# A two-layer transformer block on one core: token rows dispatched by a table of slots, an opening with routing among the wide products, and a first pass with seven inner products for three of seven weights

## The chip, the cores and the metric

The kernel runs on one core of one Trainium2 chip. The metric is the device time of one execution in microseconds (us), and the median of several runs is given. Everything is 32-bit floating point. The engines are named as in the profile: PE is TensorE (PEld its weight loads), DVE is VectorE, ACT is ScalarE, POOL is GpSimd, and SP is SyncE, which issues most DMAs.

## The reference

The block has two layers over 8 x 256 tokens of 512 channels. In outline:

```python
xn = layernorm(x)
x  = x + L0_attention(xn) + L0_experts(xn)
xn = layernorm(x)
x  = x + L1_attention(xn) + L1_low_rank(xn)
```

L0_attention is a decaying linear attention with 32 heads of 128: `qkv = silu(xn @ qkv_w.T)`, scores of each head times a decay, the result divided by its root mean square, times `norm_w`, times `sigmoid(xn @ gate_w.T)`, and projected by `out_w`. L0_experts is

```python
gate = top-2 of 16 experts, chosen within the best 2 of 4 groups
y = sum over experts e of gate[:, e] * (silu(xn @ w1[e] + b1[e]) * (xn @ w2[e] + b2[e]) @ w3[e] + b3[e])
z = silu(xn @ sw1 + sb1) * (xn @ sw2 + sb2) @ sw3 + sb3          # shared, for all tokens
```

L1_attention is a softmax attention with one head of 128 per sequence. L1_low_rank picks 16 of 64 rank-16 pairs for each token and sums their outputs with softmax weights.

## The kernel before, in words

The 2048 tokens are handled as 4 chunks (index i, NCH = 4) of 512 tokens, each of 4 tiles of 128 (index t).

**The opening** (up to `opening.close()`, L525) normalises every chunk (`begin`, L417), turns its tiles by TensorE transposes (`turn_rows`, L240), forms on POOL the sums of token blocks that the later products need (`token_sums`, L369; stored to xc, for chunk 0 kept on chip as first_x), computes the shared expert's first half (`shared_up`, L317: 16 products with 512 columns, L312), the routing (`route`, L265: 16 narrow products into ps_sc at L271, then a chain of DVE instructions), decay tables (L359) and, one chunk later, the shared expert's second half (`shared_down`, L329). In `shared_down` the chunk's gates, with a 17th column of ones, are turned by TensorE (L333), copied to geT, and multiplied with b3_t (17 x 512, the experts' biases and the shared one, L338), so that all output biases are added there; two products a tile (L340) follow. `clear` writes zeros over xd, a DRAM array with one row of 512 for every slot (47 tiles of 128 slots). After the last chunk the slot of each token's two experts is counted (L447 to L523), on DVE and with three TensorE products.

**The attention of layer 0** runs over 4 chunks x 8 groups of 4 heads. One (chunk, group) is a unit. The products of a unit are formed by a two-level scheme with seven instead of eight products: seven outer products (ORDER = p1, p2, p6, p5, p3, p7, p4), each with its own sum of weight blocks w and of token blocks x. In chunks 1 to 3 each outer product is again done with seven inner products of four 128-column matmuls (`p1` to `p7` in class Outer, `product` L661), whose operands are sums made earlier. In chunk 0, the first pass, it is done plainly (`plain`, L981): four quarters of two products, eight in all. During the first pass, POOL also makes the inner sums of each weight (`inner_sum`, L634) and stores them to DRAM (ws), from where the later chunks load them; the outer sums (p6, p5, p3, p7) are made on DVE (`outer_sum`). p1, p2 and p4 (RAW) use weights as they come. A weight tile is 8 x 512 columns (`big`, a ring of three buffers); `prepare(n + 2)` loads the weight of the outer product after next, and `following.step` runs one sum of the next weight after each product.

**Order.** Within the attention, ACT and POOL execute in the order of the code; for PE, DVE and SP a planner sets the order from its own costs. Besides, the code counts slots: `slot()` advances after a product (49 a unit), and `later(n, f)` puts a piece of other work n slots ahead. Pieces are the scores, the attention, the output projection, the routed experts (`expert`), and in the first pass the dispatch (`row`, `scatter`): a normalised tile is loaded from xnd, and POOL writes its rows by two indirect DMAs to their slots in xd. From chunk 1 on, each of 47 expert tiles loads its rows from xd (L696, on SP) and its expert's weights by an indirect DMA (L697, on POOL), turns the rows (8 slots later), does the first half (11) and the second (14); ACT copies the result and SP stores it to yd (L733, L734). `load_sum` (L933) fetches x plus the shared expert of a chunk when its last group is nearly done, and `finish` adds the attention to it.

**Layer 1** begins with `wrapped_up` (L1145), which gathers chunk 0's expert rows, adds and normalises them during the last units. `Head` (L1302) does routing and attention, `seven` the low-rank products.

Of the kernel before, what the change touches and what calls it, by code (L numbers as in the profile page):

```python
# [9 lines left out]
FP = mybir.dt.float32  # L10
I32 = mybir.dt.int32
# [55 lines left out]
def block_kernel(  # L67
# [75 lines left out]
    def once(shape, name):  # L143
        return work.tile(shape, FP, tag=name, name=name, bufs=1)

    scratch = big("scratch").rearrange("p (h b) n -> p h (b n)", h=4)
    xs = [work.tile([P, TPC, C], FP, tag="x", name=f"x{i}", bufs=NCH) for i in range(NCH)]
    x_t = x.rearrange("(i t p) c -> i t p c", t=TPC, p=P)
    for t in range(TPC):
        nc.sync.dma_start(out=xs[0][:, t, :], in_=x_t[0, t])  # L150
# [14 lines left out]
    b3_t = held[0 : E + 1, SH * C : (SH + 1) * C]  # L165
    nc.sync.dma_start(out=b3_t, in_=b3)
# [8 lines left out]
    xd = dram.tile([NSLOT, C], FP, name="xd")  # L175
# [7 lines left out]
    xnd = [dram.tile([P, TPC, C], FP, name=f"xnd{i}") for i in range(NCH)]  # L183
# [5 lines left out]
    zero = held[:, (SH + 1) * C : (SH + 2) * C].unsqueeze(1)  # L189
    nc.gpsimd.memset(zero, 0.0)  # L190

    ident = const.tile([P, P], FP, name="ident")
    make_identity(nc, ident)
    eps_t = const.tile([P, 1], FP, name="eps_t")
    nc.gpsimd.memset(eps_t, EPS)
# [5 lines left out]
    before = once([P, E, E], "before")  # L201
# [8 lines left out]
    dist = const.tile([P, S + P], FP, name="dist")  # L210
# [15 lines left out]
    def normalize(o, xc):  # L226

        mv = small.tile([P, TPC, 2], FP, tag="mv", name="mv")
        for t in range(TPC):
            st = small.tile([P, 6], FP, tag="st", name="st")  # L230
            nc.vector.bn_stats(st, xc[:, t, :])
            nc.vector.bn_aggr(mv[:, t, :], st)
        rstd = small.tile([P, TPC], FP, tag="rstd", name="rstd")
        rsqrt(rstd, mv[:, :, 1])
        for t in range(TPC):
            nc.vector.tensor_scalar(
                o[:, t, :], xc[:, t, :], mv[:, t, 0:1], rstd[:, t : t + 1], ALU.subtract, ALU.mult
            )
# [26 lines left out]
    def route(xT, ge, sel):  # L265

        full = [P, TPC, E]
        pl = ps_sc()
        for t in range(TPC):
            for c in range(NC):  # L270
                mm(  # L271
                    pl[:, bass.ts(t, E)], xT[:, c, bass.ts(t, P)], rw[:, c, :],
                    start=(c == 0), stop=(c == NC - 1),
                )
# [31 lines left out]
        tt(ge[:, :, 0:E], sc, sel, ALU.mult)  # L306
        nc.vector.memset(ge[:, :, E : E + 1], 1.0)
# [9 lines left out]
    def shared_up(i):  # L317
        hT = scratch[:, 2 + i % 2, :].rearrange("p (e n) -> p e n", e=SH)
        for e in range(SH):
            p1, p2 = ps_mm(), ps_mm()  # L320
            project(p1, wsh, e, i)
            project(p2, wsh, SH + e, i)
            h1 = work.tile([P, CH], FP, tag="h1", name="h1")
            b1, b2 = bsh_t[:, 0, e : e + 1], bsh_t[:, 1, e : e + 1]
            nc.scalar.activation(h1, p1, AF.Silu, bias=b1)
            nc.vector.scalar_tensor_tensor(hT[:, e, :], p2, b2, h1, ALU.add, ALU.mult)
        return hT

    def shared_down(i, hT):  # L329
        xc = xs[i]  # L330
        pg = ps_sc()
        for t in range(TPC):
            nc.tensor.transpose(pg[0 : E + 1, bass.ts(t, P)], gates[i][:, t, :], ident)  # L333
        gT = work.tile([E + 1, CH], FP, tag="geT", name="geT", bufs=1)
        nc.scalar.copy(gT, pg[0 : E + 1, :])
        for t in range(TPC):
            py = ps_mm()
            mm(py, gT[:, bass.ts(t, P)], b3_t, start=True, stop=False)  # L338
            for e in range(SH):
                mm(py, hT[:, e, bass.ts(t, P)], w3sh[:, e, :], start=False, stop=(e == SH - 1))  # L340
# [4 lines left out]
    sel_all = once([P, NTT, E], "sel_all")  # L345

    def share(i, hT):
        shared_down(i, hT)
        nc.sync.dma_start(out=xr[i], in_=xs[i])
# [17 lines left out]
    first_x, first_w = {}, []  # L367

    def token_sums(i):  # L369
# [18 lines left out]
        for p, at in (  # L388
# [9 lines left out]
            if i == 0:  # L398
                if y is not with_:
                    nc.sync.dma_start(out=blocks(first_x[p][:, 0:4]), in_=y)  # L400
# [9 lines left out]
    def clear(i):  # L410
        lo, hi = (0, 12, 24, 36, NMT)[i : i + 2]
        nc.sync.dma_start(
            out=xd[lo * P : hi * P, :].rearrange("(j p) c -> p j c", p=P),
            in_=zero.to_broadcast([P, hi - lo, C]),
        )

    def begin(i):  # L417
        xns.append(work.tile([P, TPC, C], FP, tag="xn", name=f"xn{i}"))
        normalize(xns[i], xs[i])
# [3 lines left out]
    for i in range(NCH):  # L423
# [3 lines left out]
        nc.sync.dma_start(out=xnd[i], in_=xns[i])  # L427
# [8 lines left out]
        ups.append(shared_up(i))  # L436
        ge = once([P, TPC, E + 1], f"ge{i}")
        route(xT[i], ge, sel_all[:, bass.ts(i, TPC), :])
        gates.append(ge)
        decays(i)  # L440
        clear(i)
# [8 lines left out]
    disp = Parts(accp.tile([P, 7 * CH], FP, tag="acc", name="disp"))  # L450
# [50 lines left out]
    nc.vector.tensor_reduce(own, owner, AX.X, ALU.add)  # L501
    nc.vector.tensor_scalar(own, own, float(E - 1), float(P), ALU.min, ALU.mult)
# [14 lines left out]
    for n in range(TOP):  # L517
        tt(hit, slot, ends_[:, n, :].unsqueeze(2).to_broadcast(full), ALU.is_equal)
        tt(hit, hit, sel_all, ALU.mult)
        for i in range(NCH):  # L520
            at_i = bass.ts(i, TPC)
            tt(hit[:, at_i, :], hit[:, at_i, :], gates[i][:, :, 0:E], ALU.mult)
# [72 lines left out]

    def spare8():
        return staged("spare")[:, 0 : TPC * C].rearrange("p (t c) -> p t c", t=TPC)

    with tc.tile_pool(name="attn", bufs=1) as attn, tc.manual_schedule(engines={mybir.EngineType.Activation, mybir.EngineType.Pool}):
# [5 lines left out]
        def weights(i, g, p, steps):  # L605
# [14 lines left out]
            if i == 0:  # L620
# [13 lines left out]
                def inner_sum(f, o, a_, b_):  # L634
                    f(w[:, o], w[:, a_], w[:, b_], pool)
                    if o == 7:
                        nc.sync.dma_start(out=ws[g][p], in_=w[:, 4 if p in RAW else 1 : 8])

                if outer:
                    steps += [partial(outer_sum, n) for n in (1, 2, 0, 3)]  # L640
                steps += [
                    partial(inner_sum, *at) for at in ((add, 4, 0, 3), (sub, 5, 4, 1), (sub, 6, 2, 5), (sub, 7, 1, 0))
                ]
# [978 lines left out]
```

## Time and profile before

| | |
|---|---|
| median of 3 runs | 2861.57 us (2854.19 to 2862.28) |
| the profiled execution | 2856.16 us, its span 2854.4 us |
| granted PE clock over the span | 0.993 |
| opening, until the first product of L666 | 164.4 us |
| first pass (chunk 0), about | 598 us |
| chunks 1 to 3 and layer 1 | from 762 us on |
| DMA | 763.21 MB, 267 GB/s on average |

The span runs from the first to the last instruction of the program in one profiled execution. Busy time is what an engine's instructions take; PE's records overlap[...], so a row of them is priced from start to start. One fp32 matmul of 512 columns shows as two records.

### The profile page before, as it was taken

To read this page: it belongs to the slowest core of one execution; us is meant where nothing else is said; L and a number is where in the kernel's file an instruction comes from. 1 tells how busy PE (TensorE), PEld (TensorE's weight loads), DVE (VectorE), ACT (ScalarE), POOL (GpSimd) and SP (SyncE) were. 2 spreads that over 40 slices of the span, in tenths; PEclk is the share of its full clock that TensorE was granted. 3 is DMA by queue.
4 is the path that set the end of the run, shared out by engine and by line. 5 is a ranking of instruction groups with operands and counts; after the bars stand their busy time and mean duration, and the time that the engine had idled before them with its cause. 6 is when DMAs were issued, how large, how long until landed. Compare 5 with 4: busy or idle time off the path is not lost. (4 is left out here: it accounts for less than half of the span.)

```text
span 2854.4 us, 49572 instructions
## 1 busy us (share of the span) xinstructions
PE 2796.7 (98%) x19864; PEld 2566.1 (90%) x19864; DVE 1569.7 (55%) x2615; ACT 948.2 (33%) x1683; POOL 1465.7 (51%) x1213
## 2 busy tenths in 40 slices
PE   8989999999999999999999999999999999999999
PEld 4469999999999999999999999999999999987877
DVE  6555666666654445444545555555555555556663
ACT  3312222212244333333443333443444333432221
POOL 4545666665546555555645454545544566552210
PEclk9999999999999999999999999999999999999999
DMA  7888998899986777778877777777777788652211
GB/s 255 301 309 337 357 352 341 341 349 347 364 320 246 262 266 273 282 270 299 296 265 257 264 266 265 259 274 280 284 259 259 267 310 298 222 212 88 76 61 61
DMA packets 161943, 763.21 MB, mean 267 GB/s; under 512 B 18209, under 2 KB 24225, under 8 KB 109874
## 3 DMA queue, kind: packets, MB, share of 16 engines
q1 hardware_dynamic: 149826, 706.25, 66.9%
q0 software_dynamic: 11888, 53.79, 5.2%
q8 instruction: 157, 2.57, 0.4%
q14 instruction: 72, 0.59, 0.1%
HBM read 596.14 MB, written 163.05 MB: 266 GB/s over the span
## 5 line engine op out<-in xcount | busy, mean ns | idle before, releaser
L666 PE MATMUL ps_a<-xt,w 128*128 128x128 f32 x5376 | 750.9, 276 | 11.7 <-DVE r L97 7.7
L666 PEld LDWEIGHTS ps_a<-xt,w 128*128 128x128 f32 x5376 | 681.9, 192 | 30.1 <-issue 14.3
L97 POOL TENSOR_TENSOR c<-c 128x512 f32<-128x512 f32 x216 | 271.7, 1273 | 262.0 <-DVE c L97 259.9
L97 POOL TENSOR_TENSOR c<-c,r 128x512 f32<-128x512 f32 x240 | 318.4, 1347 | 158.9 <-DVE r L97 153.1
L666 PE MATMUL ps_e<-xt,w 128*128 128x128 f32 x2688 | 373.4, 275 | 1.3 <-DVE c L97 1.3
L97 POOL TENSOR_TENSOR sums<-sums,sq 128x512 f32<-128x512 f32 x120 | 153.3, 1278 | 426.4 <-ACT sq L796 425.6
L996 ACT COPY cp<-ps_a 128x512 f32<-128x512 f32 x336 | 196.4, 585 | 476.0 <-PE ps_a L666 468.8
L666 PEld LDWEIGHTS ps_e<-xt,w 128*128 128x128 f32 x2688 | 344.4, 192 | 11.2 <-issue 3.8
L97 POOL TENSOR_TENSOR w<-w 128x512 f32<-128x512 f32 x224 | 294.6, 1325 | 108.2 <-issue 31.2
L666 PE MATMUL ps_a<-w,xt 128*128 128x128 f32 x1792 | 346.7, 275 | 0.0
L858 PE MATMUL ps_sc<-wo,gT 128*128 128x256 f32 x1288 | 305.1, 379 | 1.8 <-POOL gT L97 1.8
L97 DVE TENSOR_TENSOR acc<-ps_sc,acc 128x512 f32<-128x512 f32 x208 | 143.3, 690 | 265.8 <-PE ps_sc L858 198.8
L666 PEld LDWEIGHTS ps_a<-w,xt 128*128 128x128 f32 x1792 | 272.3, 192 | 0.0
L97 DVE TENSOR_TENSOR c<-ps_a,c 128x512 f32<-128x512 f32 x232 | 157.9, 686 | 202.7 <-PE ps_a L666 201.7
L858 PEld LDWEIGHTS ps_sc<-wo,gT 128*128 128x128 f32 x1288 | 232.3, 190 | 26.8 <-POOL gT L97 2.0
L666 PE MATMUL ps_b<-xt,w 128*128 128x128 f32 x1680 | 236.4, 277 | 6.8 <-ACT c L1010 4.2
L801 DVE SCALAR_TENSOR_TENSOR gT<-ps_o,nw,c 128x256 f32<-128x256 f32 x256 | 112.0, 479 | 231.0 <-ACT sq L796 222.0
L666 PEld LDWEIGHTS ps_b<-xt,w 128*128 128x128 f32 x1680 | 217.3, 194 | 17.5 <-issue 8.2
L744 ACT ACTIVATE c<-c 128x512 f32<-128x512 f32 x256 | 148.9, 627 | 170.1 <-DVE c L97 170.0
L796 ACT ACTIVATE sq<-ps_o 128x512 f32<-128x512 f32 x120 | 71.6, 597 | 382.3 <-PE ps_o L782 382.3
L666 PE MATMUL ps_e<-w,xt 128*128 128x128 f32 x896 | 173.2, 275 | 0.0
L97 DVE TENSOR_TENSOR s<-ps_sc,decay 128x384 f32<-128x384 f32 x256 | 139.8, 552 | 40.7 <-PE ps_sc L770 38.1
(299 smaller groups left out, 4635.8 us busy)
## 6 DMA issues: line engine op xcount, KB each, us to landing
w<-in_w_att_dram SPq DMA_DIRECT2D x128, 1024.0 KB
st<-in_w_att_dram SPq DMA_DIRECT2D x32, 1024.0 KB
wo<-in_w_out_dram SPq DMA_DIRECT2D x113, 256.0 KB
decay<-dec SPq DMA_DIRECT2D x64, 384.0 KB
w<-ws0p SPq DMA_DIRECT2D x12, 1792.0 KB
w<-ws1p SPq DMA_DIRECT2D x12, 1792.0 KB
w<-ws2p SPq DMA_DIRECT2D x12, 1792.0 KB
w<-ws3p SPq DMA_DIRECT2D x12, 1792.0 KB
```

The costliest lines, as they stand in the source:

```text
L97: (eng or nc.vector).tensor_tensor(o, a, b, op)
L666: mm(bank[:, bass.ts(ty, P)], a, b, start=(first and ty == 0), stop=True, skip_group_check=True,)
L744: nc.scalar.activation(qk, qk, AF.Silu)
L796: nc.scalar.activation(sq, po, AF.Square)
L801: nc.vector.scalar_tensor_tensor(gT[:, h, :].rearrange("p (t n) -> p t n", t=2), po[:, bass.ts(h, S)].rearrange("p (t n) -> p t n", t=2), ...
L858: mm(py[:, bass.ts(t, S)], self.O[p][:, hh, bass.ts(t, P)], self.wo[p][:, hh, :], start=(t == 0 and hh == 0), stop=(hh == 1), skip_group_c ...
L996: nc.scalar.copy(c, bank)
```

## The change

1. **Dispatch.** The array xd and its clearing go. xnd becomes one array of 2048 rows; a new DRAM array `table` (one 32-bit number for each slot, declared last) is set to 0, and in the first pass POOL scatters token numbers into it: 32 indirect DMAs of 128 numbers in place of 16 row loads and 32 scatters of rows. At the last unit of the pass `read_table` loads the table, and TensorE turns it (`whose`). Each expert tile then gathers its rows from xnd by an indirect DMA on POOL.
2. **Biases.** b3_t, the gates' transposes and the product L338 go. An expert tile gathers its bias row by another indirect DMA (own_, 12 slots after its begin) into the place of its rows, and DVE adds it to the product (before: a copy on ACT). Pieces lie at 10, 12, 13 and 18 slots instead of 8, 11 and 14. The shared bias is added by `last_bias`: a load and four POOL adds for each chunk.
3. **Opening.** The loads of chunk 0 alternate between the queues of SP and ACT, its tiles are normalised one at a time, an early square root and 16 transposes of the identity are added, the routing's products stand between the shared expert's (`between`), and the next chunk is turned ahead of this chunk's decays and of `share`. sel_all, before and the gates move into disp (the space of acc), dist into the opening's pool.
4. **First pass.** p1, p2 and p4 use seven inner products, as the later chunks do; p6, p5, p3 and p7 stay plain (`sevenfold`). The inner sum for p7 is made first, and the token sums of chunk 0 for these three are made by 12 POOL instructions on 128 x 128 blocks (`first_sums`). A seven's last product, `p3`, stands after the next outer product's first two, or ahead of a plain one.
5. **Layer 1.** `wrapped_up` normalises in pieces, and the first head's routing products stand between those of q and k (`opening`).

```diff
-    b3_t = held[0 : E + 1, SH * C : (SH + 1) * C]
-    nc.sync.dma_start(out=b3_t, in_=b3)
-        nc.sync.dma_start(out=xs[0][:, t, :], in_=x_t[0, t])
+        (nc.scalar if t % 2 else nc.sync).dma_start(out=xs[0][:, t, :], in_=x_t[0, t])
...
+    table = dram.tile([NSLOT, 1], I32, name="table")
+    none = once([NMT, P], "none", I32)
+    nc.gpsimd.memset(none, 0)
+    nc.sync.dma_start(out=table.rearrange("(j p) o -> j (p o)", p=P), in_=none)
...
+    nc.scalar.activation(root[:, 0:1], eps_t, AF.Sqrt)
+    for _ in range(2):
+        idle = ps_o()
+        for n in range(WARM):
+            nc.tensor.transpose(idle[:, bass.ts(n % 4, P)], ident, ident)
...
         for t in range(TPC):
-            nc.tensor.transpose(pg[0 : E + 1, bass.ts(t, P)], gates[i][:, t, :], ident)
-        gT = work.tile([E + 1, CH], FP, tag="geT", name="geT", bufs=1)
-        nc.scalar.copy(gT, pg[0 : E + 1, :])
-        for t in range(TPC):
             py = ps_mm()
-            mm(py, gT[:, bass.ts(t, P)], b3_t, start=True, stop=False)
...
+        pl, tiles = ps_sc(), list(range(TPC))
+        ups.append(shared_up(i, lambda: scores(pl, xT[i], tiles.pop(0))))
+        ge = disp.tile([P, TPC, E], FP, name=f"ge{i}")
+        route(pl, ge, sel_all[:, bass.ts(i, TPC), :])
         gates.append(ge)
+        if i + 1 < NCH:
+            turn(i + 1)
         decays(i)
-        clear(i)
...
+    def last_bias(r, t3):
+        nc.sync.dma_start(out=t3, in_=b3[E : E + 1].to_broadcast([P, C]))
+        for t in range(TPC):
+            add(r[:, t, :], r[:, t, :], t3, nc.gpsimd)
...
                 steps += [
-                    partial(inner_sum, *at) for at in ((add, 4, 0, 3), (sub, 5, 4, 1), (sub, 6, 2, 5), (sub, 7, 1, 0))
+                    partial(inner_sum, *at) for at in ((sub, 7, 1, 0), (add, 4, 0, 3), (sub, 5, 4, 1), (sub, 6, 2, 5))
                 ]
+                if p in RAW:
+                    return sums_of(w)
...
+        for t in first_sums:
+            sub(t[:, 4], t[:, 1], t[:, 0], nc.gpsimd)
+            sub(t[:, 1], t[:, 3], t[:, 1], nc.gpsimd)
+            sub(t[:, 5], t[:, 3], t[:, 4], nc.gpsimd)
+            sub(t[:, 6], t[:, 2], t[:, 5], nc.gpsimd)
...
-                nc.sync.dma_start(out=self.xe, in_=xd[bass.ts(j, P), :])
+                nc.gpsimd.indirect_dma_start(
+                    out=self.xe, out_offset=None, in_=xnd[:, :],
+                    in_offset=bass.IndirectOffsetOnAxis(ap=whose[:, j : j + 1], axis=0),
+                    bounds_check=NT - 1, oob_is_err=False,
+                )
...
+            def bias(self):
+                nc.gpsimd.indirect_dma_start(
+                    out=self.xe, out_offset=None, in_=b3[:, :],
+                    in_offset=bass.IndirectOffsetOnAxis(ap=own_[:, self.j : self.j + 1], axis=0),
+                    bounds_check=E, oob_is_err=False,
+                )
...
-                nc.scalar.copy(ye, py)
+                add(ye, py, self.xe)
...
+                    last_bias(self.r, attn.tile([P, C], FP, tag="sum", name="sb3", bufs=3))
...
             def go(self, bank, p, first=False):
                 product(bank, self.w[p], self.x[p], first)
                 slot()
+                if self.following:
+                    self.following.step()
...
-            later(8, e.turn)
-            later(11, e.up)
-            later(14, e.down)
+            later(10, e.turn)
+            later(12, e.bias)
+            later(13, e.up)
+            later(18, e.down)
...
+        def sevenfold(n):
+            return plan[n][0] > 0 or plan[n][2] in RAW
...
-                    for e in range(2):
-                        later(1 + 24 * e, partial(row, 2 * g + e))
+                    for e in range(5 * g, min(5 * g + 5, TOP * NTT)):
+                        later(5 + 10 * (e - 5 * g), partial(scatter, e // TOP, e % TOP))
+                    if g == NG - 1:
+                        later(4, read_table)
...
-            if i == 0:
+            last = outers[n - 1] if n and sevenfold(n - 1) else None
+            if not sevenfold(n):
+                if last:
+                    last.p3()
                 prepare(n + 2)
                 cur.plain(outers[n + 1])
                 continue
+            if i == 0:
+                while cur.steps:
+                    cur.step()
+                cur.following = outers[n + 1]
             cur.p1()
             cur.p7()
-            if plan[n - 1][0] > 0:
-                outers[n - 1].p3()
+            if last:
+                last.p3()
             prepare(n + 2)
```

## The prediction

> **What bounds the kernel now.** I read the page first, then the busy time by stage (cut where the records change code lines), TensorE's list of waits, and the records themselves in time order.
>
> ```profile
> span 2854.4 us, 49572 instructions
> PE 2796.7 (98%) x19864; PEld 2566.1 (90%) x19864; DVE 1569.7 (55%) x2615; ACT 948.2 (33%) x1683; POOL 1465.7 (51%) x1213
> ```
>
> TensorE is busy 98%, the next engine 55%. Removed matmuls are therefore worth about their time, if their feeders keep up. By stage (columns: window, length, busy us and instructions of PE, PEld, DVE, ACT, POOL, granted clock, DMA share, GB/s):
>
> ```profile
> 0.00:164.40 164.40, 144.23 (x439) 73.60 (x439) 96.32 (x201) 53.09 (x79) 81.94 (x129) 0.94 0.75 279
> 164.40:762.00 597.60, 584.73 (x4527) 564.38 (x4526) 371.37 (x587) 128.71 (x222) 351.05 (x275) 0.99 0.90 344
> 762.00:1457.00 695.00, 692.09 (x5286) 657.38 (x5285) 347.48 (x538) 276.39 (x498) 383.63 (x302) 1.00 0.77 285
> ```
>
> The opening idles 20 us, the first pass 13 (most of it in its first unit), the second 3. The waits (total us, times, longest) name the places:
>
> ```profile
> PE ps_b L243 <- DVE xn L236: 10.2, 1, 10.2
> PE ps_b L666 <- ACT c L1010: 4.2, 1, 4.2
> PE ps_sc L333 <- DVE ge L97: 3.6, 1, 3.6
> ```
>
> TensorE's records in time order (start, duration): eight wide records (L312) take 5.44 us from start to start early on and 3.43 soon after; the L338 pairs further down are those that the change removes:
>
> ```profile
> 13.66 5.14 PE L271 MATMUL ps_sc<-rw,xT 128*128 128x16 f32 x24
> 18.63 5.60 PE L312 MATMUL ps_b<-xT,wsh 128*128 128x512 f32 x8
> 24.07 3.60 PE L312 MATMUL ps_a<-xT,wsh 128*128 128x512 f32 x8
> 27.50 3.60 PE L312 MATMUL ps_e<-xT,wsh 128*128 128x512 f32 x8
> ...
> 131.91 1.12 PE L338 MATMUL ps_b<-held,geT 17*128 17x512 f32 x2 [0.67 <-ACT geT L335]
> 132.96 1.98 PE L340 MATMUL ps_b<-held,scratch 128*128 128x512 f32 x4
> 134.87 1.12 PE L338 MATMUL ps_a<-held,geT 17*128 17x512 f32 x2
> ```
>
> Prices are start to start, since records overlap: L312 3.43 us per eight, L338 1.05 per pair, L340 1.91 per four.
>
> **The Trainium skill.** "TensorE: Matmul & The Clock Gate", Part 1: the array starts at half clock and is released after about 3.4 us of activity. The trace agrees in kind (the first transposes come every 0.22 us, later ones every 0.11), although its clock column says 1.00 there. "DMA: Bandwidth & Descriptors", Anatomy of one DMA: a GpSimd-issued DMA costs about 2.0 us plus bytes over 436 GB/s, an estimate of 2.6 us for 256 KB. The trace disagrees: 256 KB row gathers (L556) land after a median 6.2 us, row scatters (L1094) after 7.3. "ScalarE: Activation LUTs", What ACT_TABLE_LOAD costs: 1283 ns; the trace shows 1.28 us at 7.68, on the chain to the first transpose.
>
> **The opening (−45 us).** Removed: the biases b3 through TensorE. 16 pairs x 1.05 = 16.8; 16 gate transposes, about 4 x 0.45 = 1.8; their waits on geT (2.0) and ge (3.6). Added ahead: x on two queues, statistics, root and scaling per tile, a table load done early, 16 idle transposes. The statistics of the last tile of x began at 6.72; with 0.69 + 0.18 + 0.30 + 0.18 + 0.54 and hand-overs it is scaled near 9, turned and copied near 10. The wide products, which need the 1 MB w_sh issued at 4.09, started at 18.63; I put them at 10 (x and w_sh, 2 MB at the 287 GB/s of that stretch from about 2.5, is 9.8). What remains for TensorE: L312 16 x 3.43 = 54.9; L340 16 x 1.91 = 30.6; scores 4 x 1.71 = 6.8; transposes of three chunks 5.3; counting 1.7: 99.3, so 109.3 with no idle. Cold stretches and waits were about 28 us here; turning a chunk ahead and scores between products take most of those at 36 to 43, 74 to 85 and 147 to 155. I keep 10: the opening ends at 119, 45 earlier. DVE still has 95 us of work there, so it becomes nearly as tight as TensorE. The 12 MB clearing of xd goes (DMA share 0.75, so worth nothing by itself, but the xsum stores behind it held POOL 47.5 us). If DVE's cover fails, the opening is DVE's, which is rival 2. The set-up edits (table, none, own_, token, dist's place, the order of memsets) are records of 0.1 to 0.5 us on POOL and DVE and two 24 KB transfers, beside a first transpose that waits for x anyway: nothing. ACT issues two of the x loads ahead of its first work.
>
> **Entry into the first pass (−5 us).** ACT's first copy of c waited for DVE's counting to 175.33, for its memory was the opening's; sel_all, before and the gates now lie in disp. That returns most of the 4.2 us wait, the 1.7 us on w at 186.7 and a cold 1.5. Of 7.4 I take 5, since p6's 3 MB must still come.
>
> **The first pass (−13 us).** By the diff only p1, p2 and p4 get seven products, not all seven outer ones: one of 8 products, 3 x 8 times. A product is 0.89 us (563.42 to 564.32), so 24 x 0.89 = 21.4. ACT and DVE gain 6 copies and 3 adds a unit (3.5 and 2.1 us), POOL 6 adds (7.8 of about 47 busy in 74.5, plus twelve small sums once): hidden by idle time (uncovered, POOL's would be 8 x 7.8 = 62 us). But products now need POOL's inner sums of w, which were only stored before. Worst is p4 (first pass, sixth unit, whose p1 begins at 537.64 and the next at 612.09: 74.45 us; SPq rows are issues):
>
> ```profile
> 589.31 6.36 SPq L622 DMA_DIRECT2D w<-in_w_att_dram  x2
> 599.74 5.21 POOL L97 TENSOR_TENSOR w<-w 128x512 f32<-128x512 f32 x4 [2.85 <-issue]
> 602.32 0.83 PE L666 MATMUL ps_b<-xt,w 128*128 128x128 f32 x6
> ```
>
> Its load waits for a buffer whose store ends at 589.3, and lands at 599.7; the sums p7 and p6 need are ready at 601.0 and 603.7, while TensorE reaches p4 at 602.32 and, 1.8 us less for p1 and p2, would want them near 601.4 and 602.6. A last product after the next two also returns p4's buffer about 0.9 us later. Against this, 2 row loads and 4 scatters a unit (1.5 of about 26 MB: 344 GB/s x 74.5 us) become 512-byte scatters: some 2 us off the 39 us of DMA in this ring. I take a stall of 1 us a unit: 8 x (2.7 − 1) = 13. Bounds 0 and 21.4. Scatters no longer wait for a row on POOL.
>
> **Passes two to four (+5 us).** Each of 47 tiles gets two more indirect DMAs on POOL, and loses one load on SP:
>
> ```profile
> L697 POOL DMA_INDIRECT xw<-in_w_exp_dram,rows__1106 x47: 1005/1011/1053, 764.0 to 2211.2; - x47
> ```
>
> 94 x 1.0 us lies in POOL's idle 45%. The result's bias add moves from ACT (0.58) to DVE (0.69), 32 us on an engine half idle. The new wait: the bias gather is issued 12 slots after the tile's begin, needed at 18. A unit of 49 slots takes 73.1 us, 1.49 a slot, so 9 us for a landing of 6 to 7.5 plus POOL's delay (0 to 5 us: L697 at 1072.26 followed ten back-to-back POOL records). DVE then waits up to about 3 us for some tiles, with the sc bank held and every product's eviction queued behind; TensorE is late when its a, b and e banks are all unread. Bounds 0 and 117 (47 x 2.5); I take 5. On POOL the gather also waits for the tile's own transposes, two slots before it. The later turn (10 for 8) gives the token gather time.
>
> **Shared bias, closing (0).** last_bias: a 256 KB load and four POOL adds of 1.27 before finish, four times; its t3 needs a sum buffer, on SP, and POOL's c adds queue behind. The 1 MB r was issued at 768.3 and used at 801, so only t3 can be late: 0 to 5 each, I take +3 in all. Splitting the normalisation in wrapped_up takes the 2.6 us wait at 2443, and interleaving ranks with q and k some of the 0.4 there: −3.
>
> **Sum.** −45 − 5 − 13 + 5 + 3 − 3 = −58. The profiled execution took 2856.16 (span 2854.4 and 1.8 around it): 2798. The median is 5.4 above it, so 2804.
>
> **Rivals.** (1) All of it: no cold stretch (−52), full 21, no costs: about 2780. For it: POOL and DVE have the time; against: the p4 lines. (2) Feeders bind: DVE's chain of chunk after chunk ends the opening at 138 (−26) and the ring of three weight buffers keeps the first pass at 74.5 us a unit (0): about −26, 2835. For it: DVE 96 us of 119, DMA 0.90 in the pass; against: 12 and 12.6 MB less to move. (3) Slower: the bias gather stops DVE in Expert.down. From 58/47 = 1.2 us a tile it eats the gain; at 2.5 the time is about 2920. For: landings up to 13.0 us at L697; against: the 256 KB gathers landed within 8.9 us at worst, and POOL waits for others half its time, so is mostly on time. That all seven outers take the seven form is only the title; the code leaves four plain.
>
> **How the numbers follow.** Forecast 0.52, rival 1 0.13, rival 2 0.20, rival 3 0.12 (nearly all slower), small mixtures near no change 0.03. Forecast and rivals 1 and 2 span 2780 to 2835; with the bounds of the opening (±8) and runs (8 us apart before) 2768 to 2846, which leaves out 0.15. Differences under 0.3% (8.6 us) can't be told from none: faster 0.84, same 0.03, slower 0.13.
>
> **What would show it.** Right: no L338-like records; first wide product near 10 and first pass product near 119; units of the first pass near 73 us; the remaining stages within 10 us of 2093. Wrong: TensorE waiting for POOL's w at p4; DVE waiting for the bias gather; POOL held in last_bias; an opening that ends past 135 with DVE as releaser.

## The result, and the profile after

The changed kernel takes 2941.73 us (median; 2934.31 to 2950.83). The kernel before, run beside it, takes 2861.58 us (2854.19 to 2862.28). The ratio is 1.0288, with a 95% interval of 1.0252 to 1.0323: it is slower by 80 us, where the forecast was 2804 us. The profiled execution took 2938.48 us.

The page's head (the span, then busy time, share and instructions of each engine):

```profile
span 2936.8 us, 49479 instructions
PE 2777.3 (95%) x19641; PEld 2560.4 (87%) x19641; DVE 1641.1 (56%) x2689; ACT 947.0 (32%) x1682; POOL 1651.0 (56%) x1383
```

TensorE is busy 19 us less than before (2796.7) in a span that is 82 us longer. The removed matmuls are gone; what was added is mostly idle time, and in part matmuls that take longer (the first experiment separates the two). The busy time by stage shows where. The columns are the window, its length, busy us and instructions of PE, PEld, DVE, ACT and POOL, granted clock, DMA share, and GB/s. The stages here are cut at the first product, at the first gather of an expert's weights (the first slots of the second pass), and at the last product.

```profile
0.00:131.90 131.90, 114.45 (x401) 65.06 (x401) 96.75 (x193) 48.85 (x77) 87.71 (x141) 0.95 0.72 268
131.90:828.80 696.90, 595.43 (x4376) 568.38 (x4377) 402.62 (x628) 157.23 (x272) 417.20 (x326) 0.93 0.93 276
828.80:2609.60 1780.80, 1755.68 (x13363) 1671.63 (x13362) 952.69 (x1427) 677.46 (x1207) 1072.63 (x858) 1.00 0.76 278
```

Cut at the same marks, the kernel before has 164.4, 599.6, 1768.3 and, from the last product on, 322.1 us. The changed kernel has 131.9, 696.9, 1780.8 and 327.2. So the opening gave 32.5 us, the first pass took 97.3, the other passes 12.5 and the rest 5.1.

In the first pass the DMA share rose from 0.90 to 0.93 while the rate fell from 344 to 276 GB/s. The DMA engines are no less busy and deliver a fifth less. TensorE's list of waits (total us, times, longest) says what it lacks:

```profile
PE ps_a L710 <- DMA w<-in_w_att_dram: 46.5, 6, 10.2
PE ps_a L710 <- DVE w L98: 13.4, 6, 5.5
PE ps_o L844 <- DVE s L98: 11.1, 5, 7.6
PE ps_b L710 <- DVE w L98: 9.4, 1, 9.4
PE ps_sc L779 <- DVE xeT L763: 9.0, 7, 1.3
```

None of these was among the waits that the prediction showed of before. The first, second and fourth are for weights that are late, or for sums made from them; the third lies in the same stage. All fall in the first pass except the fifth, which is in the second.

One answer on the records of the new scatter names a suspect. Its lines give the duration (in ns), the idle time of POOL for an earlier scatter that had not landed (us, times), and the time from issue to landing:

```profile
L1156 POOL DMA_INDIRECT table<-token,slots x32: 992/993/1699, 143.6 to 704.3; - x32
  DMA table<-token,slots: 25.3, 6
DMA to landing us min/median/max: 9.7/11.1/13.8
```

512 bytes take 11.1 us to land. A scatter of 256 KB of rows in the kernel before took 7.3 (L1094):

```profile
DMA to landing us min/median/max: 6.7/7.3/8.2
```

The trace also records every DMA packet. In the changed kernel 461 packets take over 2.5 us, together 1706 us, or 107 us for each of the 16 DMA engines. In the kernel before there are 3, together 8 us. 411 of the 461 begin 3 to 9 us after a scatter, though these stretches are 192 of the 561 us from the first scatter to the last, and every one of the 32 scatters has some. After the scatter at 253.12 us, for instance, 16 packets of 14336 bytes begin between 258.73 and 258.88 and take 2.9 to 6.5 us each; the mean of that size in the first pass of the kernel before is 0.56.

### The profile page after: what moved, and what is told of

Its sections match the earlier page's. It is cut to its first block, busy times and chain, and to the rows that moved or that the text cites. A ratio compares the mean times of both kernels' runs of the same rounds, so it can differ in the third digit from the quotient of the medians.

```text
span 2936.8 us, 49479 instructions
## 1 busy us (share of the span) xinstructions
PE 2777.3 (95%) x19641; PEld 2560.4 (87%) x19641; DVE 1641.1 (56%) x2689; ACT 947.0 (32%) x1682; POOL 1651.0 (56%) x1383
## 4 chain that ended last, share of the span: by engine, by line
PE 71%; DMA 14%; DVE 8%; issue 4%; POOL 3%; SPq 0%; ACT 0%; DVEq 0%; POOLq 0%; ACTq 0%
PE ps_a L710 20%; PE ps_e L710 10%; PE ps_sc L921 9%; PE ps_b L710 5%; DMA st<-in_w_att_dram 4%; PE ps_o L844 3%; PE ps_sc L832 3%; PE ps_sc L779 3%; DMA w<-in_w_att_dram 3%; PE ps_sc L941 2%; PE ps_a L1633 2%; DVE w L98 2%; PE ps_o L845 2%; PE ps_sc L833 1%; DVE r L98 1%
## 5 line engine op out<-in xcount | busy, mean ns | idle before, releaser
L710 PE MATMUL ps_a<-xt,w 128*128 128x128 f32 x5376 | 762.1, 278 | 74.9 <-DMA w<-in_w_att_dram 46.5
L710 PEld LDWEIGHTS ps_a<-xt,w 128*128 128x128 f32 x5376 | 695.0, 194 | 103.5 <-issue 59.6
L98 POOL TENSOR_TENSOR c<-c 128x512 f32<-128x512 f32 x240 | 302.5, 1276 | 263.1 <-DVE c L98 254.0
L98 POOL TENSOR_TENSOR c<-c,r 128x512 f32<-128x512 f32 x264 | 347.7, 1337 | 174.0 <-DVE r L98 171.7
L1063 ACT COPY cp<-ps_a 128x512 f32<-128x512 f32 x384 | 224.1, 584 | 659.1 <-PE ps_a L710 631.7
L710 PE MATMUL ps_b<-xt,w 128*128 128x128 f32 x1536 | 218.6, 279 | 21.0 <-DVE w L98 9.4
L98 DVE TENSOR_TENSOR c<-ps_a,c 128x512 f32<-128x512 f32 x216 | 146.9, 687 | 144.7 <-PE ps_a L710 138.9
L710 PEld LDWEIGHTS ps_b<-xt,w 128*128 128x128 f32 x1536 | 199.3, 195 | 29.7 <-issue 27.8
```

The lines of the kernel that those rows point to most:

```text
L98: (eng or nc.vector).tensor_tensor(o, a, b, op)
L710: mm(bank[:, bass.ts(ty, P)], a, b, start=(first and ty == 0), stop=True, skip_group_check=True,)
L1063: nc.scalar.copy(c, bank)
```

## Experiments: what stopped the first pass

Three theories stood at first. Theory S: the scatters of single numbers hold up every DMA beside them. Theory P: the arrays lie elsewhere in DRAM now and collide. Theory R: the form of seven waits for POOL's sums and the ring of three weight buffers. Four kernels ran on one chip, beside 2857.41 us for the kernel before.

**No scatter.** The changed kernel without its 32 scatters. The table is filled with spread numbers, so that tiles gather rows of other tokens.

```diff
-    nc.gpsimd.memset(none, 0)
+    nc.gpsimd.iota(none, pattern=[[1, P]], base=0, channel_multiplier=37)
         def scatter(t, n):
-            nc.gpsimd.indirect_dma_start(out=table[:, :], ...)
+            return
```

> The changed kernel with its 32 scatters of token numbers left out; the table holds other, spread token numbers from the start, so the expert tiles gather the wrong rows. Theory S (each scatter of 128 four-byte numbers holds up all DMA queues for some 5 us): no packet of the first pass takes over 2.5 us, the first pass falls from about 696 us to 570 to 600, time 2820 to 2850. Theory P (the arrays lie elsewhere in DRAM now that xd is gone, and collide): nothing changes, 2930 to 2950. Theory R (the seven-product form waits for POOL's sums and the ring of three weight buffers): little changes, 2910 to 2945.

Measured: 2828.59 us, ratio 0.9899 (0.988 to 0.9918), and 2 packets over 2.5 us. Its first pass (columns as above):

```profile
135.10:721.60 586.50, 573.04 (x4376) 551.04 (x4377) 404.38 (x628) 156.74 (x273) 385.28 (x293) 0.99 0.87 327
```

The medians of the changed kernel with and without the scatters differ by 113 us, 3.5 us a scatter. Without them the rate is 327 GB/s, the granted clock 0.99 and the stage 586.5 us: 13.1 less than before the change, and 110.4 less than with them, close to the 107 us of long packets per engine. Theories P and R, by which little would change, fail. Of the 110.4 us, 88.0 are idle time of TensorE (101.5 against 13.5), and 22.4 are the same number of recorded products taking longer in all (595.43 against 573.04).

**The same scatters in the kernel before.** Its dispatch stays; after each scatter of rows comes one of 128 four-byte numbers into a table that nothing reads.

```diff
+    table = dram.tile([NSLOT, 1], I32, name="table")
         def scatter(x_, t, n):
             ...
+            nc.gpsimd.indirect_dma_start(
+                out=table[:, :],
+                out_offset=bass.IndirectOffsetOnAxis(ap=slots[:, n, t : t + 1], axis=0),
+                in_=slots[:, n, t : t + 1], in_offset=None, ...)
```

> The kernel before with one scatter of 128 four-byte numbers into a table of its own after each of the 32 row scatters; nothing reads the table. Theory S: slower by 70 to 110 us, 2930 to 2970, all of it in the first pass. Theories P and R: slower by 0 to 5 us (32 more instructions of 1.0 us on a POOL that is half idle), 2860 to 2867.

Measured: 2986.07 us, ratio 1.0451 (1.0423 to 1.0479). That is 129 us more, against 70 to 110 expected. By stage the first pass, in which all 32 scatters run, takes 711.1 us: 111.5 more, or 3.5 a scatter, as in the changed kernel. The trace has 503 packets over 2.5 us, 112 us per engine. Of the rest, 11.1 us lie in the opening, before the first scatter, at a granted clock of 0.87 against 0.94; no run says why. So neither the seven form nor the placement of the changed kernel is needed for the stall.

**Rows again.** The changed kernel with the dispatch of before (xd, its clearing, row loads and row scatters, tiles loaded by SP).

```diff
-    table = dram.tile([NSLOT, 1], I32, name="table")
+    xd = dram.tile([NSLOT, C], FP, name="xd")
...
-                        later(5 + 10 * (e - 5 * g), partial(scatter, e // TOP, e % TOP))
+                        later(1 + 24 * e, partial(row, 2 * g + e))
```

> The changed kernel with the dispatch of before: xd, its clearing, 16 row loads, 32 scatters of 256 KB of rows, and expert rows loaded by SP. All else as changed. Theory S: the first pass is freed of the stalls; with the opening still some 30 us shorter the time is 2815 to 2850. Theory P: also 2815 to 2850, since xd is back in its place (with the run that leaves the scatters out, the two are told apart). Theory R: 2910 to 2945.

Measured: 2870.62 us, ratio 1.0043 (1.0026 to 1.006), a miss. The trace has one packet over 2.5 us, so the stall is gone; but two other waits of TensorE stand in the list:

```profile
PE ps_a L717 <- DVE r L98: 27.3, 24, 4.9
PE ps_a L717 <- ACT cp L1066: 25.5, 1, 25.5
```

At the end of the opening ACT's first cp waits 40.9 us for the store of xr, and the 12 MB clearing, put back among these stores, is the likely reason. In the first pass DVE's r waits 24.1 us for row scatters that still hold its ring of buffers. The kernel before orders this work so that neither shows; the changed one does not. The comparison therefore says what rows cost in this order, not what they cost in general.

**Numbers 512 bytes apart.** The same 32 scatters of 128 numbers, into places 128 numbers apart. The part that is read back is filled with spread numbers, so tiles gather rows of other tokens.

```diff
-    table = dram.tile([NSLOT, 1], I32, name="table")
+    table = dram.tile([NSLOT * P, 1], I32, name="table")
+    nc.vector.tensor_scalar(apart, ends_, float(P), None, ALU.mult)
-                out_offset=bass.IndirectOffsetOnAxis(ap=slots[:, n, t : t + 1], axis=0),
+                out_offset=bass.IndirectOffsetOnAxis(ap=apart[:, n, t : t + 1], axis=0),
```

> The changed kernel with the same 32 scatters of 128 four-byte numbers, but the numbers of neighbouring slots 512 bytes apart in a table 128 times as long; the part that is read back is filled with other, spread numbers, so the expert tiles gather the wrong rows. If the stall comes from many numbers in one line of DRAM (neighbouring slots): as without scatters, 2820 to 2850. If it comes from each small write by itself: no change, 2930 to 2950. I hold the first for likelier, 0.6.

Measured: 2831.3 us, ratio 0.9905 (0.9889 to 0.9922), one packet over 2.5 us. As many scatters of as many bytes cost next to nothing. It is not the smallness of the writes alone, but that the slots of one expert's tokens follow one another, so that a scatter puts numbers 4 bytes apart. How many it puts so can be worked out from the reference's router: for six seeds of its inputs two or three experts take most of the tokens, and on average 97 to 126 of the 127 steps between the sorted slots of one scatter are single slots. Most of the 128 numbers of a scatter then stand next to one another, in a few runs. Which draw the measured kernels had is not on record.

**Two shorter distances.** Is it enough that the numbers are not neighbours, or must each have 512 bytes to itself? One kernel puts them 64 bytes apart (rows of other tokens again). The other keeps the 24 KB table of 6016 numbers and turns its order: slot s goes to (s mod 128) x 47 + s div 128. Neighbouring slots are then 188 bytes apart, and the table is read straight into `whose`, without TensorE's transpose. These kernels, and two of the next part, ran beside 2856.65 us for the kernel before. The first diff is against the kernel with 512 bytes, the second against the changed one.

```diff
-    nc.vector.tensor_scalar(apart, ends_, float(P), None, ALU.mult)
+    nc.vector.tensor_scalar(apart, ends_, 16.0, None, ALU.mult)
```

> The changed kernel with numbers 64 bytes apart instead of 4 (rows gathered for other tokens, so the output is not the reference's). Theory N (neighbours within one short line): 2828 to 2836 us, as with 512 bytes. Rival L (the same 512 bytes): some eight numbers of an expert in one scatter fill 512 bytes then, as with 4 bytes apart, so most of the loss stays, 2890 to 2945 us.

```diff
+    nc.vector.tensor_scalar(where, slots, 7, None, ALU.logical_shift_right)
+    nc.vector.tensor_scalar(apart, slots, P - 1, None, ALU.bitwise_and)
+    nc.vector.scalar_tensor_tensor(apart, apart, float(NMT), where, ALU.mult, ALU.add)
-            nc.sync.dma_start(out=rows[0:NMT], in_=table.rearrange("(j p) o -> j (p o)", p=P))
+            nc.sync.dma_start(out=whose, in_=table.rearrange("(p j) o -> p (j o)", p=P))
```

> The changed kernel with the table's order turned: the number of slot s stands at (s mod 128) x 47 + s div 128, so that neighbouring slots lie 188 bytes apart in the same 24 KB, and the table is read straight into place, without TensorE's transpose. Theory N (numbers of neighbouring slots side by side make the stall; any distance of a line of some tens of bytes is enough): 2827 to 2836 us, as with numbers 512 bytes apart, no run of packets over 2.5 us. Rival L (several numbers of one scatter within the same 512 bytes make it): two or three numbers then still share 512 bytes, and the time lies between, 2850 to 2920 us.

Measured: 64 bytes, 2835.15 us, ratio 0.992 (0.9893 to 0.9948), with one packet over 2.5 us. Turned, 2833.28 us, ratio 0.9912 (0.9883 to 0.9941), with 3. The turned kernel's scatter:

```profile
L1161 POOL DMA_INDIRECT table<-token,apart x32: 994/996/1912, 146.0 to 600.3; - x32
DMA to landing us min/median/max: 2.4/5.8/8.0
```

Theory N, that neighbouring places make the stall, holds: 64 bytes are enough, and the landing falls from 11.1 to 6.0 us (5.8 in the turned table). The turned table is as large as the changed kernel's, so its size is not the cause. In it only the slots of one expert are sure to lie apart; a number of another expert can still fall nearer than 188 bytes, so the kernel with 64 bytes is the cleaner measure of the distance. The turned kernel leaves nothing out and is faster than both kernels. What happens between 4 and 64 bytes was not tried, nor is it shown what in the memory or the DMA engines makes the stall.

## Experiments: the rest of the gap

With the stall gone the kernel gains 21 to 29 us, not 58. The profiles' stages, at the same marks (us):

| kernel | opening | first pass | passes 2 to 4 | rest | span |
|---|---|---|---|---|---|
| before | 164.4 | 599.6 | 1768.3 | 322.1 | 2854.4 |
| the change | 131.9 | 696.9 | 1780.8 | 327.2 | 2936.8 |
| no scatter | 135.1 | 586.5 | 1780.2 | 326.0 | 2827.8 |
| 512 bytes apart | 133.7 | 589.8 | 1781.8 | 327.4 | 2832.7 |
| turned | 133.4 | 592.3 | 1783.1 | 326.2 | 2835.1 |
| plain first pass | 131.7 | 600.1 | 1777.7 | 326.3 | 2835.8 |
| turn at 8 | 134.4 | 589.4 | 1798.4 | 327.7 | 2849.9 |
| first half at 14 | 134.0 | 585.8 | 1770.1 | 325.5 | 2815.4 |
| no biases | 133.6 | 588.5 | 1776.2 | 326.4 | 2824.8 |
| copies first | 127.0 | 591.7 | 1780.0 | 326.6 | 2825.4 |
| all three mends | 127.3 | 589.0 | 1772.1 | 326.5 | 2814.9 |

**What the seven form is worth in the first pass.** The kernel with numbers 512 bytes apart, and p1, p2 and p4 of the first pass plain again.

```diff
-            return plan[n][0] > 0 or plan[n][2] in RAW
+            return plan[n][0] > 0
```

The sums that only the form of seven needs go with it (not shown).

> The kernel with numbers 512 bytes apart (rows gathered for other tokens, so the output is not the reference's), and the first pass plain throughout, as before the change. Theory F (the form of seven for three weights is worth the 21.4 us of its 24 products less 1 us of stalls a unit): slower by 13 us, about 2844 us (2840 to 2853). Rival R (the ring of three weight buffers sets the first pass's units, and the gain of 10 to 13 us there came from the row loads and row scatters that went): no slower, 2828 to 2834 us.

Measured: 2837.54 us, ratio 0.9929 (0.9906 to 0.9951); with the seven form it was 0.9905 (0.9889 to 0.9922). The whole times can't be told apart, but the stages can be read: the first pass takes 600.1 us against 589.8, so the form gains 10.3 us there. TensorE is busy 17.7 us less in that stage (588.1 without the form, 570.4 with it) and idle 7.4 more (12.0 and 19.4). The other profiles with the form and a table, but without the stall, have 585.8 to 592.3 us for this stage, so the 10.3 are uncertain by some 4. 4 us come back in passes two to four, for which no run gives a reason. In the turned kernel TensorE waits for POOL's w 3.4 us in all (4 times); the stall put into the sum was 8.

**The second pass.** The units' starts (the first multiplication by the decay in each) lie mostly 75.9 us apart before, and mostly 77.3 in the changed kernel. One such unit, in the kernel with numbers 512 bytes apart; first TensorE, then DVE (start, duration, instruction, idle time before it):

```profile
790.94 0.60 PE L763 MATMUL ps_sc<-ident,xw 128*128 128x128 f32 x4
...
796.40 2.05 PE L781 MATMUL ps_sc<-xeT,xw 128*128 128x128 f32 x16 [1.29 <-DVE xeT L765]
```

```profile
792.28 3.47 DVE L98 TENSOR_TENSOR c<-c,r 128x512 f32<-128x512 f32 x2
795.67 0.68 DVE L765 COPY xeT<-ps_sc 128x512 f32<-128x512 f32 x1
```

The tile's rows are turned at 791, but their copy stands on DVE behind two adds of c. The first half comes 3 slots later and waits 1.29 us. Three kernels test this. The first puts the turn, the bias gather and the first half back to 8, 10 and 11 slots (numbers 512 bytes apart).

```diff
-            later(10, e.turn)
-            later(12, e.bias)
-            later(13, e.up)
+            later(8, e.turn)
+            later(10, e.bias)
+            later(11, e.up)
```

> The kernel with numbers 512 bytes apart (rows gathered for other tokens, so the output is not the reference's), and of each expert tile the turn, the bias gather and the first half put back to 8, 10 and 11 slots; the second half stays at 18. Theory Q (in the second pass the copy of the turned rows stands on DVE behind two adds of c, because turn and first half fall on bad slots; 7 waits of 1.28 us): those waits go and the units of the second pass return from 77.3 to 75.9 us, so about 2820 us (2817 to 2824). Rival B (the bias itself, its gather and the add on DVE, costs the 12 us of passes two to four): 2829 to 2835 us.

Measured: 2851.19 us, ratio 0.9977 (0.9967 to 0.9988): a miss in size and sign. The waits for xeT left the head of the list, and this took their place:

```profile
PE ps_sc L763 <- DMA xw<-xnd,whose: 19.3, 9, 3.7
```

The gather of token rows runs on POOL, and at 8 slots it has not always landed when TensorE turns. So the 10 slots are needed, and the test had to move the other side: the first half alone goes to 14. This and the next two are made from the turned kernel and ran together, beside 2856.7 us for the kernel before.

```diff
-            later(13, e.up)
+            later(14, e.up)
```

> The changed kernel with the turned table (numbers 188 bytes apart), and the first half of each expert tile one slot later, at 14 instead of 13. Theory Q (seven times in the second pass the first half stands on TensorE until DVE, busy with two adds of c of 1.7 us, has copied the turned rows, 1.28 us each): a slot is about 1.5 us, so these waits go, units of the second pass 75.9 us, about 2824 us (2820 to 2828). Rival M (a piece that is moved a slot meets another full place): 2830 us or more, with other waits in their place.

Measured: 2819.65 us, ratio 0.9866 (0.9845 to 0.9888), against 2833.28 for the turned table alone. No wait for xeT is left among TensorE's waits, the second pass's units are 75.8 us, and passes two to four take 1770.1 us, 1.8 more than before the change; every profile with the first half at 13 and the turn at 10 has 1776 or more. Theory Q, that the slots cost the second pass its time, holds, with 13 us rather than 9: some start and end units of the later passes gain as well (83.9 us became 80.0 at the head of the third).

**The biases.** The turned kernel, with the experts' biases left out (no gather, and ACT's copy in place of DVE's add).

```diff
-            later(12, e.bias)
-                add(ye, py, self.xe)
+                nc.scalar.copy(ye, py)
```

> The changed kernel with the turned table, and the experts' biases left out: no gather of the bias rows, and ACT copies the result of a tile as before the change, in place of DVE's add. Theory Q (the slots, not the bias, cost passes two to four their 12 us): 2828 to 2836 us, units of the second pass stay near 77.3 us. Rival B (the bias costs it): 2818 to 2825 us, with units of 75.9 us.

Measured: 2830.02 us, ratio 0.9902 (0.988 to 0.9924), units of the second pass 77.4 us. The bias is not the cause of the longer units. DVE does wait for its rows in the turned kernel (15.0 us, 5 times), but TensorE hardly feels it: the stage is 6.9 us shorter in the one profile, and the medians differ by 3 with intervals that overlap.

**The opening.** It ended at 131.9 us where 119 was forecast. The records of the changed kernel around the first wide product (start, duration, instruction, idle time before it); first DVE:

```profile
12.40 0.69 DVE L245 BATCH_NORM_STATS2 st<-x 128x6 f32<-128x512 f32 x1 [2.39 <-DMA x<-in_x_dram]
...
13.80 0.67 DVE L276 COPY xT<-ps_b 128x512 f32<-128x512 f32 x1
14.39 0.68 DVE L276 COPY xT<-ps_e 128x512 f32<-128x512 f32 x1
```

Then TensorE:

```profile
9.92 1.06 PE L271 MATMUL ps_a<-ident,xn 128*128 128x128 f32 x4
...
14.53 3.68 PE L295 MATMUL ps_sc<-rw,xT 128*128 128x16 f32 x20 [2.12 <-DVE xT L276]
18.05 5.75 PE L339 MATMUL ps_b<-xT,wsh 128*128 128x512 f32 x8
```

The tiles are turned near 10, as forecast. But DVE's copies of the last two are queued behind the statistics of chunk 1, which wait for the load of x. In the experiment DVE's work on chunk 1 is queued behind these copies.

```diff
-            nc.vector.tensor_copy(o, i)
+            copies_.append(nc.vector.tensor_copy(o, i))
...
+        if i == 0:
+            with tc.issue_after(copies_[-1].ins):
+                begin(1)
+        elif i + 1 < NCH:
             begin(i + 1)
```

> The changed kernel with the turned table, and in the opening DVE's work on the second chunk of x queued behind its copies of the first chunk's turned tiles. There the copies stood from about 10.3 to 15.6 us behind statistics that wait for the second chunk's load, and the first wide product began at 20.3 us. Theory O (that order makes the late start of the wide products, and the opening is TensorE's): wide products from about 16 us, the opening ends 4 us earlier, near 129.5 us, in all about 2829 us. Rival D (from 40 to 80 us the opening is DVE's anyway): the wide products start earlier, but the end moves by less than 1.5 us, 2831 to 2835 us.

Measured: 2826.67 us, ratio 0.9891 (0.9868 to 0.9913). TensorE there:

```profile
13.16 3.20 PE L295 MATMUL ps_sc<-rw,xT 128*128 128x16 f32 x24
16.21 3.68 PE L339 MATMUL ps_b<-xT,wsh 128*128 128x512 f32 x8
```

The opening ends at 127.0 us, 6.4 earlier than in the turned kernel. The whole times of the two overlap in their intervals, so the reading is the stage's: the profiles with the old order and a table end their openings between 131.7 and 135.6 us, the two with the copies first (this one and the next) at 127.0 and 127.3. Theory O, that the order made the late start, holds and gives more than the 4 us expected: the first eight wide products now take 3.68 us, and not 5.75. So DVE's order at one place set at least these 6 us of the opening.

**All three mends together** (beside 2857.0 us for the kernel before):

```diff
             nc.sync.dma_start(out=whose, in_=table.rearrange("(p j) o -> p (j o)", p=P))
...
-            later(13, e.up)
+            later(14, e.up)
...
+            with tc.issue_after(copies_[-1].ins):
```

> The changed kernel with all three mends: the turned table (numbers 188 bytes apart), the first half of an expert tile at 14 slots, and DVE's copies of the first chunk's turned tiles ahead of its work on the second chunk. Theory O and Q together (the two places have nothing in common, so the gains of 13.6 and 6.6 us against the turned table alone add up): 2813 us (2809 to 2817). Rival T (the end of the opening only meets another wait in the first pass): 2817 to 2822 us, as the first half at 14 alone.

Measured: 2816.67 us (2814.92 to 2817.35), ratio 0.985 (0.9829 to 0.9871). It lies at the upper edge of what theories O and Q gave and at the lower edge of rival T, and its interval overlaps that of the first half at 14 alone. The stages show that the opening kept its gain (127.3 us) and the second pass its own (units of 75.8); the first pass took 3.2 us more and the later ones 2.0 more than with the first half at 14 alone. Single executions scatter by as much (the profiled one of the first half at 14, 2817.14, lies 2.5 us under its median), so whether a wait stands behind it stays open.

## Why the prediction was wrong

The step that failed stands in **the first pass (−13 us)**: "2 row loads and 4 scatters a unit (...) become 512-byte scatters: some 2 us off the 39 us of DMA in this ring". A transfer was priced by its bytes, and fewer bytes were counted as a relief of the ring of weight buffers. The trace of before had no scatter of single numbers, so nothing there gave a price, and the bounds of 0 and 21.4 us were set for the products alone. The runs put the cost of the 32 scatters in the first pass at 110.4 us in the changed kernel and 111.5 us in the kernel before. Nor is the relief to be seen: with harmless scatters and plain products the stage took 600.1 us, against 599.6 before the change.

The span was forecast 58 us shorter and came out 82 longer. Of these 140 us, 115 lie in the entry and the first pass, and 110 of them are the scatters.

The other steps, apart from this:

- **Opening, −45:** −32.5 in the profile. The removed pairs and transposes are gone. "I put them at 10" was wrong: 18.05. The bandwidth sum had x and w_sh there by 9.8 us, and "turned and copied near 10" was half right: tiles were turned, but the last two copies began at 13.80 and 14.39. Three tiles' routing products also stand ahead of the first wide one; they are in the sum of 99.3, but not ahead of the start. From the first wide product on, TensorE was idle 10.0 us, just what was kept (7.9 of it in one wait, for the second chunk's scratch on DVE), and busy 103.9 where 99.3 was forecast for the whole. Mending the order gave 6.4 of the missing 12.9 us.
- **Entry −5 and first pass −13:** without the scatters 599.6 became 586.5, which is −13 for both together, where −18 was forecast, and −7 to −11 in three profiles with harmless scatters (512, 64 and 188 bytes apart). The seven form gives 10.3 in its experiment, inside its bounds of 0 to 21.4 and close to 13. It has the shape of the forecast, too: 17.7 us of products gone where 21.4 was put, and 7.4 us of idle time added where 8 was put. But POOL's w at p4 is only part of that idle time (3.4 us in the turned kernel). What is left for the entry is next to nothing: with plain products the wait for ACT's c fell from 4.2 to 1.1 us, and waits for DVE's gT in the same pass grew from 2.8 to 6.6.
- **Passes two to four, +5, and shared bias, +3:** +12.5. The sign was right and the reason mostly wrong. The forecast looked for the cost in the bias gather; 13 us were the turned rows' copy on DVE, met by the first half at slot 13: the turn had moved from 8 to 10 and the first half from 11 to 13. last_bias was not measured apart.
- **Closing, −3:** the 2.6 us wait is gone and the last unit is 5.0 us shorter (72.6 to 67.6), but that lies before the last product; from there on the kernel takes 5.1 us more (322.1 to 327.2). The largest wait there, for DVE's cp, grew from 1.8 to 4.8 us. No experiment was made on it.

Of the rivals, the third had the sign for another reason: the bias gather, of which next to nothing reached TensorE. The second, an opening near 138 and no gain in the first pass, gave 2835, which the turned table meets (2833) by luck, for its parts were others: the opening was better than it said, the first pass gained, and the second pass lost. The signs of failure that the prediction listed did not name this one: it listed waits of one engine for another, and no rate of DMA beside its share.

## What to carry to other kernels

Price a new DMA by where its pieces land as well as by its bytes: in this kernel single numbers scattered next to one another held up the transfers beside them, and turning the order of the table cured it for three small DVE instructions. When the DMA share stays high and the GB/s fall, look at the time from issue to landing of whatever small transfer is new. When slots or queues are rearranged, ask of each turned tile who copies it and what stands before that copy in its engine's order; two such places cost 6 and 13 us here, and each was cured in a few lines.

## What the runs showed of the hardware that was not expected

- A scatter of 128 four-byte numbers, most of them 4 bytes apart, landed after a median 11.1 us, and packets of other transfers took up to 7.3 us beside it, where the two sizes most often held up took 0.35 and 0.59 on average before the change. It cost 3.5 us of the first pass each time, in two kernels. With the numbers of neighbouring slots 64, 188 or 512 bytes apart it landed after 5.8 to 6.1 us and cost nothing that can be told from none.
- The granted TensorE clock of the first pass was 0.93 with the stalls and 0.99 without them, the products being the same: with the waits came a lower clock, and the products took 22.4 us longer in all. The column is no full account of it: from 18.63 to 24.07 us of the kernel before it says 1.00, while eight wide records took 5.44 us, against 3.43 just after.
